# Sums by source in half buckets side by side, and another order of the node steps at the stages' ends

## The chip, the cores and the metric

The kernel runs on one core of a Trainium2 chip. The metric is the time of one execution on the device in microseconds, the median of several runs; lower is better. Names of engines: PE (matrix multiply), DVE (vector), ACT (scalar), POOL (gathers and scatters by index), SP (issues the plain DMAs, in order).

## The reference

Four graph layers follow each other on the same 6250 nodes (rows of 160 numbers: 64 scalars and 32 three-vectors) and the same 100000 edges (`src`, `dst`, sorted by `dst`). Every layer normalizes the node rows, mixes them linearly, forms a message for each edge from the row of one end and from weights that a small network makes of the edge's features, sums the messages over the edges of each node, mixes the sums and adds them to the rows. Layers 0, 1 and 3 read the row of `src` and sum by `dst`. Layer 2 does the opposite, it reads the row of `dst` and sums by `src`, and the edges aren't sorted by `src`:

```python
xs = s[dst]; xv = v[dst]
out0a = w0 * xs                              # and four more products
tp = jnp.concatenate([out0a, out0b, out1a.reshape(E, -1), out1b.reshape(E, -1), out1c.reshape(E, -1)], axis=-1)
agg = jax.ops.segment_sum(tp, src, num_segments=N) / DENOM
```

## The kernel before

The program runs through these stages, one after the other.

- **The start** (lines 740 to 880): the node rows are normalized and mixed for layer 0, in 50 tiles of 128 rows (`nodes_in`). Beside it the sort by `src` begins: `src_b` holds each edge's bucket, `src // 120`, and for each of the 53 buckets (and one for the padding) `count_bucket` (L760, L763) compares `src_b` with the bucket's number and counts, on DVE and partly on ACT (L765). From the counts come `start2`, where each bucket begins, and `off`. A flag tells whether the data keep within what the fast program is made for (among others no more than 16 x 128 edges in a bucket); only if not, the plain program `general` runs instead.
- **`edges(0)`, `edges(1)`, `edges(3)`**, the layers that sum by `dst`: 784 tiles of 128 edges, 4 to a group, so 196 groups. For each tile POOL gathers 128 rows of a table in DRAM by index (L1278), six groups ahead. PE makes the edge weights, DVE the one-hot matrices `oh` (128 edges x 64 nodes) and the messages, and PE sums them, `pg += oh.T @ msg` (L1395): the tiles of a window of 14 alternate between the upper and lower 64 rows of `pg`. A window ends with a chain of node steps, a Python generator that is advanced twice a group: `nodes_out` (transpose, output weights, add to the row), then `nodes_in` of the next layer (norm, transpose, input weights), whose row goes to the next layer's table in DRAM (L1033). The generators that are left after the last group are run one after the other. The first gather of a layer needs the whole table of that layer.
- **The sort's second half**, `positions`, another generator, which `edges(0)` and `edges(1)` advance by one step in every third group: for each bucket DVE makes `hit` (L1165), a running count over it (L1167) and takes it over where it hits (L1170). At its end `edge_to` holds for each edge its place in the order by `src`.
- **`messages2`**: layer 2's messages for each edge. PE spreads the rows of `dst` over the edges (L1482) and makes the weights, DVE forms the products, and POOL scatters each edge's record of 390 numbers to its place in `rec2` in DRAM (L1514). Before that, `tail` (L1424, L1426) writes zeros to 2048 rows behind the last edge, in four DMAs of SP, since the last buckets' loads reach beyond it.
- **`sums2`**: layer 2's sums. A bucket has 120 nodes and 16 slots of 128 records (the last one 10 nodes and 2 slots), read from `rec2` from the bucket's start on, 4 slots a load (L1575, 8 loads ahead, 12 buffers). For each slot DVE makes `oh` (128 x 120, L1606) and two products (L1610, L1612); PE does `pg += oh.T @ [record, products]` in two matmuls of 192 and 288 columns (L1616, L1618). Records of a neighbouring bucket that a load takes in match no column of `oh`. Each bucket's node steps follow (`nodes_out`, then `nodes_in` of layer 3).

Instructions are placed on each engine in an order that the framework's scheduler chooses; each engine works its own list in order, and so does SP with its DMAs, those that load and those that write.

Of the kernel before, what the change touches and what calls it, by code (L numbers as in the profile page):

```python
# [66 lines left out]
BN = 120  # L67
BK = (N + BN - 1) // BN
LASTN = N - (BK - 1) * BN
S = 16  # L70
LASTS = 2
EP = TT * P + S * P

# [616 lines left out]
class Fast:  # L690
# [5 lines left out]
    def __init__(self, tc, a, out, shared, dram):  # L696
# [6 lines left out]
        self.rec2 = dram.tile([EP, RW], F32, name="rec2")  # L703
# [3 lines left out]
    def prologue(self):  # L707
# [16 lines left out]
        self.start2 = sh.tile([1, BK], I32, name="start2")  # L724
# [5 lines left out]
        self.zeros_b = sh.tile([P, TT], BF16, name="zeros_b")  # L730
# [21 lines left out]
        nc.vector.tensor_scalar(flt, src, 1.0 / BN, 0.5 / BN - 0.5, op0=ALU.mult, op1=ALU.add)  # L752
        nc.vector.tensor_scalar(flt, flt, 12582912.0, None, op0=ALU.add)
        nc.vector.tensor_scalar(self.src_b, flt, 12582912.0, None, op0=ALU.subtract)
        count = pro.tile([P, BK + 1], F32, name="count")

        def count_bucket(b):
            hit = pro.tile([P, TT], BF16, name="hit", bufs=4)
            if b % 2:
                nc.vector.tensor_scalar(hit, self.src_b, float(b), None, op0=ALU.is_equal, op1=ALU.add,  # L760
                                        accum_out=count[:, b : b + 1])
            else:
                nc.vector.tensor_scalar(hit, self.src_b, float(b), None, op0=ALU.is_equal)  # L763
                junk = pro.tile([P, TT], BF16, name="junk", bufs=2)
                nc.scalar.activation(junk, hit, AF.Copy, accum_out=count[:, b : b + 1])  # L765

        with tc.tile_pool(name="nodes0", bufs=2) as wk, \
# [3 lines left out]
            for b in range(N0 + 4):  # L771
# [14 lines left out]
                if b < BK + 1:  # L786
# [5 lines left out]
        po = pro_ps.tile([P, 2, BK + 1], F32, name="ps_off")  # L792
        nc.tensor.matmul(po[:, 0, :], lhsT=self.before, rhs=count, start=True, stop=True)
        nc.tensor.matmul(po[:, 1, :], lhsT=self.ones, rhs=count, start=True, stop=True)
        total = pro.tile([P, BK + 1], F32, name="total")
        nc.vector.tensor_copy(total, po[:, 1, :])
        ends = pro.tile([P, BK + 1], F32, name="ends")
        nc.vector.tensor_tensor_scan(ends, total, self.zeros_b[:, : BK + 1], 0.0, op0=ALU.add, op1=ALU.add)
        nc.vector.tensor_sub(ends, ends, total)
        nc.vector.tensor_copy(self.start2, ends[0:1, :BK])  # L800
        nc.vector.scalar_tensor_tensor(self.off, ends, -1.0, po[:, 0, :], op0=ALU.add, op1=ALU.add)
# [47 lines left out]
        bad = pro.tile([1, 2, P], F32, name="bad")  # L849
# [7 lines left out]
        nc.vector.tensor_scalar(bad[:, 1, 64 : 64 + BK - 1], total[0:1, : BK - 1], float(S * P), None, op0=ALU.is_gt)  # L857
        nc.vector.tensor_scalar(bad[:, 1, 64 + BK : 65 + BK], total[0:1, BK - 1 : BK], float(LASTS * P), None,
                                op0=ALU.is_gt)
# [281 lines left out]
    def positions(self, wk):  # L1141
# [10 lines left out]
        nc.scalar.copy(rs[:, :, 0:3], sq)  # L1152
        yield
# [9 lines left out]
        for b in range(BK + 1):  # L1163
            hit = wk.tile([P, TT], BF16, name="hit2", bufs=2)
            nc.vector.tensor_scalar(hit, self.src_b, float(b), None, op0=ALU.is_equal)  # L1165
# [6 lines left out]
        nc.vector.tensor_copy(to, pos)  # L1172
# [30 lines left out]
    def edges(self, li):  # L1203
# [179 lines left out]
        for i, (u, g) in enumerate(groups):  # L1383
# [17 lines left out]
            live = [n for n in live if not (next(n, True) or next(n, True))]  # L1401
            if li < 2 and i % 3 == 0:
                next(self.sort, None)
        for n in live:
            for _ in n:
                pass
# [5 lines left out]
    def messages2(self):  # L1412
# [10 lines left out]
        tail = wk.tile([P, 4, RW], F32, name="tail", bufs=1)  # L1423
        nc.vector.memset(tail, 0.0)  # L1424
        for r in range(TT * P, EP, 4 * P):
            nc.sync.dma_start(self.rec2[r : r + 4 * P, :].rearrange("(p r) c -> p r c", r=4), tail)  # L1426
# [121 lines left out]
    def sums2(self):  # L1548

        nc, tc, li = self.nc, self.tc, 2  # L1550
        es = ExitStack()
        ld = es.enter_context(tc.tile_pool(name="ld_s", bufs=12))
# [7 lines left out]

        def slots(b):
            return S if b < BK - 1 else LASTS

        data, xts, starts = {}, {}, {}
        groups = [(b, g) for b in range(BK) for g in range(0, slots(b), G)]

        def load(b, g):

            m, n = min(G, slots(b)), BN if b < BK - 1 else LASTN
            if g == 0:  # L1570
                starts[b] = nc.values_load(
                    self.start2[0:1, b : b + 1], engines=[mybir.EngineType.SP], min_val=0, max_val=E,
                    skip_runtime_bounds_check_because="a count of edges, of which there are E")
            rt = ld.tile([P, G, RW], F32, name="rt")
            nc.sync.dma_start(rt[:, :m, :],  # L1575
                              self.rec2[ds(starts[b] + g * P, m * P), :].rearrange("(p s) c -> p s c", s=m))
            loc = ld.tile([P, G], F32, name="loc")
            nc.vector.tensor_scalar(loc[:, :m], rt[:, :m, 261], float(-BN * b), None, op0=ALU.add)
            data[b, g] = rt, loc
            if g == 0:  # L1580
                rows = slice(1 + BN * b, 1 + BN * b + n)
                xt = nk.tile([BN, XW], F32, name="xt", bufs=8)[:n]
                nc.sync.dma_start(xt, self.x[2][rows, :])
                sk = nk.tile([BN, 192], F32, name="sk_out", bufs=8)[:n]
                nc.sync.dma_start(sk, self.skip[2][rows, :])
                xts[b] = xt, sk
# [179 lines left out]
```

## Time and profile before

| | us |
|---|---|
| runs of the kernel before (3) | 5309.66 median, 5302.54 to 5310.14 |
| the profiled execution, its own time | 5299.63 |
| its span, first to last instruction | 5297.8 |
| start, until the first gather of layer 0 | 172.0 |
| `edges(0)`, first to last gather | 172.0 to 1213.5 |
| `edges(1)`, first to last gather | 1270.8 to 2304.9 |
| `messages2`, first scatter to the first load of `sums2` | 2369.0 to 3429.8 |
| `sums2`, first load to the last sum matmul | 3429.8 to about 4234.8 |
| `edges(3)`, first to last gather | 4255.8 to 5270.8 |

Over the span PE is busy 83%, DVE 78%, POOL 60%, ACT 39%; the mean clock granted to PE is 0.880. These shares are means over stages with different limits, so the stages are read one by one. Each fp32 matmul stands in the records twice (834 slots of `sums2` give 1668 records of L1618).

### The profile page before, as it was taken

The page shows a single profiled execution, that of the slowest core. Times are in us where ns is not written, and L with a number is a line of the kernel's source. Part 1 is how long each engine was busy: PE and PEld are TensorE (multiplying, and loading weights), DVE is VectorE, ACT ScalarE, POOL GpSimd, SP SyncE. Part 2 cuts the span into 40 slices and gives each one's busy share as a digit, 9 for nine tenths or more (in the row PEclk, how much of TensorE's full clock was granted, in tenths as well). Part 3 has the DMA queues.
Part 4 walks back from the last instruction along what each step waited for, and adds up shares of the span by engine and source line. Part 5 has one row for each costly group of instructions (what it writes and reads, how often), then busy time and mean ns, then how long its engine had stood idle before and what let it go on. Part 6 is the DMA issues. An engine that isn't in the chain of part 4 may idle for free. (4 is left out here: it accounts for less than half of the span.)

```text
span 5297.8 us, 77181 instructions
## 1 busy us (share of the span) xinstructions
PE 4419.6 (83%) x22084; PEld 2768.0 (52%) x22084; DVE 4113.6 (78%) x11512; ACT 2078.7 (39%) x6858; POOL 3199.1 (60%) x3143
## 2 busy tenths in 40 slices
PE   6899999998999999965555556499999988878886
PEld 4455555554555555533333334388888844444443
DVE  6688889896898988857777777577777668887787
ACT  5444445443444545523333333222222244434332
POOL 0577777774777777747777777600000067777776
PEclk9999999997998989977777777699999978898888
DMA  3333333322333333336565555487777433333322
GB/s 96 114 94 95 95 95 92 94 73 78 98 101 96 100 96 99 87 123 209 199 207 199 204 198 198 172 287 234 237 234 237 157 88 83 87 82 85 84 81 58
DMA packets 373004, 708.21 MB, mean 134 GB/s; under 512 B 71469, under 2 KB 250890, under 8 KB 372442
## 3 DMA queue, kind: packets, MB, share of 16 engines
q0 software_dynamic: 163072, 349.43, 21.7%
q1 hardware_dynamic: 208914, 353.42, 21.3%
q8 instruction: 180, 2.95, 0.2%
q14 instruction: 254, 2.08, 0.1%
q10 hardware_dynamic: 584, 0.33, 0.0%
HBM read 493.90 MB, written 209.08 MB: 133 GB/s over the span
## 5 line engine op out<-in xcount | busy, mean ns | idle before, releaser
L1278 POOL DMA_INDIRECT ge<-table,rt x2352 | 2378.3, 1011 | 1770.4 <-DMA skip<-sk 828.2
L1395 PE MATMUL pg<-msg,oh 128*64 128x384 f32 x4704 | 1041.3, 563 | 145.7 <-DVE msg L1339 106.2
L1514 POOL DMA_INDIRECT rec<-row,edge_to x784 | 820.1, 1046 | 301.6 <-issue 187.6
L1305 ACT ACTIVATE ws<-pw,rt 128x96 f32<-128x96 f32 x2352 | 693.1, 350 | 768.9 <-PE pw L1301 265.1
L1301 PE MATMUL pw<-w_w2y,hh 100*128 100x192 f32 x3136 | 675.7, 352 | 17.2 <-ACT ws L1307 14.7
L1395 PEld LDWEIGHTS pg<-msg,oh 128*64 128x64 f32 x4704 | 304.3, 148 | 685.2 <-issue 251.2
L1301 PEld LDWEIGHTS pw<-w_w2y,hh 100*128 100x128 f32 x3136 | 529.7, 200 | 226.3 <-ACT ws L1307 124.8
L1338 DVE TENSOR_TENSOR msg<-msg,bank 128x768 f32<-128x768 f32 x588 | 554.6, 943 | 0.0
L1618 PE MATMUL pg<-msg,oh 128*120 128x288 f32 x1668 | 540.7, 405 | 0.0
L1482 PE MATMUL pe<-tb,oh 64*128 64x160 f32 x1568 | 276.0, 410 | 241.4 <-ACT row L1491 239.2
L1334 DVE TENSOR_TENSOR msg<-ws,ge 128x512 f32<-128x512 f32 x588 | 401.4, 683 | 67.4 <-DMA ge<-table,rt 66.1
L1616 PE MATMUL pg<-rt,oh 128*120 128x192 f32 x1668 | 409.3, 327 | 34.1 <-DVE oh L1606 34.1
L1270 ACT ACTIVATE hh<-ph 100x1024 f32<-100x1024 f32 (+1 forms) x336 | 269.4, 802 | 417.4 <-PE pw L1294 182.6
L1331 DVE TENSOR_TENSOR pr<-ge,bank 128x384 f32<-128x384 f32 x588 | 319.4, 543 | 133.5 <-DMA ge<-table,rt 131.9
L1482 PEld LDWEIGHTS pe<-tb,oh 64*128 64x128 f32 x1568 | 208.6, 255 | 393.0 <-ACT row L1491 384.7
L1307 ACT COPY ws<-pw 128x192 f32<-128x192 f32 x1176 | 391.1, 333 | 0.0
L1267 PE MATMUL ph<-ft,w_w1r 12*100 12x512 f32 (+1 forms) x784 | 337.0, 657 | 57.5 <-ACT hh L1270 40.9
L1616 PEld LDWEIGHTS pg<-rt,oh 128*120 128x120 f32 x1668 | 297.6, 183 | 122.4 <-issue 35.3
L1507 DVE TENSOR_TENSOR row<-pw,ev 128x512 f32<-128x512 f32 x196 | 135.2, 690 | 285.3 <-ACT row L1493 271.0
L1456 PE MATMUL ph<-ft,w_w1d 128*128 128x512 f32 x224 | 170.4, 856 | 220.4 <-ACT hh L1458 197.0
L1332 DVE TENSOR_REDUCE dot<-pr 128x128 f32<-128x384 f32 x588 | 342.8, 583 | 0.1
L1339 DVE TENSOR_TENSOR msg<-ge,ws 128x384 f32<-128x384 f32 x588 | 323.0, 549 | 0.0
(485 smaller groups left out, 7278.8 us busy)
## 6 DMA issues: line engine op xcount, KB each, us to landing
rt<-rec SPq DMA_DIRECT2D x208, 780.0 KB
ge<-table,rt POOLq DMA_INDIRECT x2352
ft<-in_ft_dram SPq DMA_DIRECT2D x56, 512.0 KB
ft<-in_ft_dram SPq DMA_DIRECT2D x28, 896.0 KB
dt<-in_dst_w_dram SPq DMA_DIRECT2D x112, 224.0 KB
xt<-x SPq DMA_DIRECT2D x168, 82.0 KB
rec<-row,edge_to POOLq DMA_INDIRECT x784
rt<-in_rec_dram SPq DMA_DIRECT2D x84, 112.0 KB
```

The lines of the kernel that those rows point to most:

```text
L1278: nc.gpsimd.indirect_dma_start(out=ge[:, k, :], out_offset=None, in_=self.table[li], in_offset=bass.IndirectOffsetOnAxis(ap=rt[:, G * g + ...
L1301: nc.tensor.matmul(pw[:, i, :192], lhsT=hh[:, k + i, :], rhs=w2, start=True, stop=True)
L1305: nc.scalar.activation(ws[:, k0 + i, 0:96], pw[:, i, 0:96], AF.Copy, scale=rt[:, G * g + k0 + i, 0:1])
L1307: nc.scalar.copy(ws[:, k0 : k0 + m, 96:192], pw[:, :m, 96:192])
L1332: nc.vector.tensor_reduce(dot, pr.rearrange("p g c u -> p g u c"), AX.X, ALU.add)
L1334: tt(msg[:, :, AW - 64 : AW + 64].rearrange("p g (k u) -> p g k u", k=2), ws.rearrange("p g (k u) -> p g k u", k=2)[:, :, :, 0:64], e0[:, ...
L1338: tt(mvec[:, :, :, 0:64], by3(t1, 64), yv[:, :, :, None].to_broadcast([P, n, 3, 64]), ALU.mult)
L1395: nc.tensor.matmul(pg[half], lhsT=oh[:, k, :], rhs=msg[:, k, :AW], start=t % WT < 2, stop=t % WT >= WT - 2)
L1482: nc.tensor.matmul(pe[:, 2 * h + k // 2, :160], lhsT=oh[rows, (t0 + k) % WT // 2, :], rhs=tb[rows], start=True, stop=True)
L1514: d = nc.gpsimd.indirect_dma_start(out=self.rec2, out_offset=bass.IndirectOffsetOnAxis(ap=self.edge_to[:, t0 + k : t0 + k + 1], axis=0), i ...
L1616: nc.tensor.matmul(pg[:, 0:192], lhsT=oh[:, k, :], rhs=rt[:, k, 0:192], start=first, stop=end, skip_group_check=True)
L1618: nc.tensor.matmul(pg[:, 192:480], lhsT=oh[:, k, :], rhs=msg[:, k, :], start=False, stop=end, skip_group_check=True)
```

## The change

Sums by source: a bucket has 128 nodes in two halves of 64. Each half has 9 slots of its own, and starts at its own place of `rec2`, so that there are 49 buckets of 2 x 9 slots, read 3 slots of each half at a time, in two loads of 3 slots (before, one of 4). The two halves' one-hot matrices are 64 columns wide, and their matmuls write the upper and lower 64 rows of `pg`. To have both halves counted in one pass over a bucket, each edge counts 1 or 4096 (`src_v`), so the comparison of the sort becomes one of `src_b`, multiplied by `src_v` (`scalar_tensor_tensor` in place of `tensor_scalar`); a few more operations take the two counts apart at the end. The flag's conditions become those of the halves: at most 9 x 128 edges in a half, and a half's start within 500 of 1024 times its number. Since no load reaches beyond the last edge any more (the start is capped), `tail` goes.

At the stages' ends: in the last 12 groups of `edges(0)` and `edges(1)` the sort isn't advanced, in the last 4 groups of every `edges` a node generator is advanced three times in place of two, and the generators left after the last group, in `edges` and in `sums2`, are run in turns.

The diff, cut to its core:

```diff
-BN = 120
-BK = (N + BN - 1) // BN
-LASTN = N - (BK - 1) * BN
-S = 16
-LASTS = 2
-EP = TT * P + S * P
+BK = (N + P - 1) // P
+BH = (N + HN - 1) // HN
+S, SG = 9, 3
+RH = 1024
+DRIFT, BIAS = 500.0, 512.0
+SHIFT = 4096.0
...
-        self.rec2 = dram.tile([EP, RW], F32, name="rec2")
+        self.rec2 = dram.tile([TT * P, RW], F32, name="rec2")
...
+        nc.vector.scalar_tensor_tensor(flt, self.src_b, float(-P), src, op0=ALU.mult, op1=ALU.add)
+        nc.vector.tensor_scalar(flt, flt, float(HN), SHIFT - 1.0, op0=ALU.is_ge, op1=ALU.mult)
+        nc.vector.tensor_scalar(self.src_v, flt, 1.0, None, op0=ALU.add)
...
-            if b % 2:
-                nc.vector.tensor_scalar(hit, self.src_b, float(b), None, op0=ALU.is_equal, op1=ALU.add,
-                                        accum_out=count[:, b : b + 1])
-            else:
-                nc.vector.tensor_scalar(hit, self.src_b, float(b), None, op0=ALU.is_equal)
+            nc.vector.scalar_tensor_tensor(hit, self.src_b, float(b), self.src_v, op0=ALU.is_equal, op1=ALU.mult,
+                                           **(dict(accum_out=count[:, b : b + 1]) if b % 2 else {}))
+            if b % 2 == 0:
...
-            nc.vector.tensor_scalar(hit, self.src_b, float(b), None, op0=ALU.is_equal)
+            nc.vector.scalar_tensor_tensor(hit, self.src_b, float(b), self.src_v, op0=ALU.is_equal, op1=ALU.mult)
...
-            live = [n for n in live if not (next(n, True) or next(n, True))]
-            if li < 2 and i % 3 == 0:
+            left = len(groups) - i
+            live = [n for n in live if not any(next(n, True) for _ in range(2 if left > 4 else 3))]
+            if li < 2 and i % 3 == 0 and left > 12:
                 next(self.sort, None)
-        for n in live:
-            for _ in n:
-                pass
+        while live:
+            live = [n for n in live if not next(n, True)]
...
-        tail = wk.tile([P, 4, RW], F32, name="tail", bufs=1)
-        nc.vector.memset(tail, 0.0)
-        for r in range(TT * P, EP, 4 * P):
-            nc.sync.dma_start(self.rec2[r : r + 4 * P, :].rearrange("(p r) c -> p r c", r=4), tail)
...
-        ld = es.enter_context(tc.tile_pool(name="ld_s", bufs=12))
+        ld = es.enter_context(tc.tile_pool(name="ld_s", bufs=11))
...
+        M = 2 * SG
+        AHEAD = 8
...
-        groups = [(b, g) for b in range(BK) for g in range(0, slots(b), G)]
+        groups = [(b, g) for b in range(BK) for g in range(0, S, SG)]
...
-            rt = ld.tile([P, G, RW], F32, name="rt")
-            nc.sync.dma_start(rt[:, :m, :],
-                              self.rec2[ds(starts[b] + g * P, m * P), :].rearrange("(p s) c -> p s c", s=m))
-            loc = ld.tile([P, G], F32, name="loc")
-            nc.vector.tensor_scalar(loc[:, :m], rt[:, :m, 261], float(-BN * b), None, op0=ALU.add)
+            rt = ld.tile([P, 2, SG, RW], F32, name="rt")
+            for h in range(2):
+                nc.sync.dma_start(rt[:, h], self.rec2[ds(starts[b][h] + g * P, SG * P), :].rearrange(
+                    "(p s) c -> p s c", s=SG))
...
-            oh = wk.tile([P, G, BN], F32, name="oh", bufs=3)
-            tt(oh[:, :n], self.iota[:, None, :BN].to_broadcast([P, n, BN]),
-               loc[:, :n, None].to_broadcast([P, n, BN]), ALU.is_equal)
+            oh = wk.tile([P, 2, SG, HN], F32, name="oh", bufs=3)
+            tt(oh, self.iota.rearrange("p (h n) -> p h n", h=2)[:, :, None, :].to_broadcast([P, 2, SG, HN]),
+               loc.rearrange("p (h s) -> p h s", h=2)[:, :, :, None].to_broadcast([P, 2, SG, HN]), ALU.is_equal)
...
-            for k in range(n):
-                first, end = g + k == 0, g + k == slots(b) - 1
-                nc.tensor.matmul(pg[:, 0:192], lhsT=oh[:, k, :], rhs=rt[:, k, 0:192], start=first, stop=end,
-                                 skip_group_check=True)
-                nc.tensor.matmul(pg[:, 192:480], lhsT=oh[:, k, :], rhs=msg[:, k, :], start=False, stop=end,
-                                 skip_group_check=True)
+            for k in range(SG):
+                first, end = g + k == 0, g + k == S - 1
+                for o, m in ((0, 192), (192, 288)):
+                    for h in range(2):
+                        nc.tensor.matmul(pg[HN * h : HN * h + HN, o : o + m], lhsT=oh[:, h, k, :],
+                                         rhs=(msg if o else rt)[:, h * SG + k, 0:m],
+                                         start=first and o == 0, stop=end, skip_group_check=True)
...
-        for n in live:
-            for _ in n:
-                pass
+        while live:
+            live = [n for n in live if not next(n, True)]
```

## The prediction

> **What bounds the kernel now.** I read first the busy time by stretches of 100 us, one from each kind of stage; the columns are named in the first line.
>
> ```profile
> core 0: us, PE busy (x) PEld busy (x) DVE busy (x) ACT busy (x) POOL busy (x), PEclk, DMA share, GB/s
> 900.00:1000.00 100.00, 94.86 (x490) 55.11 (x488) 90.47 (x262) 49.49 (x157) 77.14 (x76) 0.95 0.33 90
> 2800.00:2900.00 100.00, 56.07 (x324) 38.89 (x322) 71.79 (x154) 34.31 (x103) 77.46 (x75) 0.77 0.60 205
> 3700.00:3800.00 100.00, 100.00 (x536) 84.41 (x535) 72.60 (x218) 21.63 (x84) 0.00 (x0) 1.00 0.71 235
> 4700.00:4800.00 100.00, 82.28 (x424) 42.64 (x425) 81.62 (x243) 40.42 (x144) 76.54 (x78) 0.91 0.31 82
> ```
>
> In the three `edges` stages and in `messages2` POOL shows the same 77%, whatever PE and DVE do. The timeline of POOL tells why:
>
> ```profile
> 1205.60 0.94 POOL L1278 DMA_INDIRECT ge<-table,rt  x1 [0.30 <-DMA ge<-table,rt]
> 1206.85 0.94 POOL L1278 DMA_INDIRECT ge<-table,rt  x1 [0.30 <-issue]
> 1270.76 0.94 POOL L1278 DMA_INDIRECT ge<-table,rt  x1 [55.90 <-PE pw L1301]
> ```
>
> A gather takes 0.94 us and the next follows after 0.30 (no gap within a layer is over 0.32), so 1.25 us a tile and 784 x 1.25 = 980 us a layer. That is the limit there; the third line shows the hole of 56 us between two layers. In `sums2` (the row of 3700) POOL is idle and PE has no free moment at full clock, so PE is the limit. SP's own waits in the stage agree: its loads wait for buffers that PE has not finished with.
>
> ```profile
> SPq L1575 <- PE pg L1616: 335.5, 158, 3.3
> ```
>
> The change works on `sums2` above all, and there on PE. The timeline of PE, first a group of four half-wide sums of `edges`, then the full-wide ones of `sums2`:
>
> ```profile
> 1216.55 1.51 PE L1395 MATMUL pg<-msg,oh 128*64 128x384 f32 x8
> 3700.55 0.49 PE L1616 MATMUL pg<-rt,oh 128*120 128x192 f32 x2
> 3700.88 0.65 PE L1618 MATMUL pg<-msg,oh 128*120 128x288 f32 x2
> 3701.36 0.49 PE L1616 MATMUL pg<-rt,oh 128*120 128x192 f32 x2
> ```
>
> A slot of 480 columns takes 3701.36 - 3700.55 = 0.81 us, 1.69 ns a column. Four half-wide matmuls of 384 columns take 1.51 us, 0.98 ns a column with the pipeline's end included; one after the other they would take 2.6. Those for the upper and the lower rows run side by side.
>
> **The change part by part.**
>
> *`sums2`, PE.* From the first load to the last sum it takes 805 us (3429.8 to 4234.8), about 8 of them the first load's way. 797 us over 52.1 buckets is 15.3 us a bucket: 16 x 0.81 = 12.96 for the sums, 2.3 for the node steps. After: 9 pairs of slots at 0.81 (half of two slots) to 0.94 us (480 x 2 x 0.98 ns). I take 0.81, since 1.51 has the end in it: 7.3 + 2.3 = 9.6 us, at most 10.8, for 49 buckets.
>
> *`sums2`, DVE.* Groups of `sums2` from 3500 to 4180 us, busy us and mean ns of one:
>
> ```profile
> L1610 DVE TENSOR_TENSOR msg<-rt 128x768 f32<-128x768 f32 x178 | 169.4, 951 | 0.0
> L1606 DVE TENSOR_TENSOR oh<-iota,loc 128x480 f32<-128x480 f32 x178 | 116.7, 655 | 75.9 <-PE pg L1618 75.2
> L1612 DVE TENSOR_TENSOR msg<-rt 128x384 f32<-128x384 f32 x177 | 97.6, 551 | 0.0
> L1578 DVE TENSOR_SCALAR loc<-rt 128x4 f32<-128x4 f32 x181 | 29.9, 165 | 94.6 <-DMA rt<-rec 94.1
> ```
>
> Neighbours overlap by about 0.08 us, so a group of four costs 2.32 - 0.32 = 2.0 us and a bucket 8.0; at 73% busy of 15.2 us the node steps have 3.0. After, six slots a group: by the slope between 384 and 768 elements (1.04 ns) the products take 1.35 (1152) and 0.75 us (576), `oh` with 384 elements 0.55 (between 407 ns for 256 in L1320 and 655 for 480), `loc` 0.165; less the overlaps 2.5 us. Three groups and the nodes: 10.5 us a bucket.
>
> *`sums2`, DMA.* Before, 834 slots of 128 x 1560 bytes are 166.5 MB; after, 49 x 18 slots, 176.1 MB. Rows in and out (`xt`, `sk`, `table`, `skip`, `x`) are 6250 x 3360 bytes, 21.0 MB: 197.1 MB. What the DMA engines can do lies between two rows, the queue from 3500 to 4200 us (MB, share of the 16 engines) and ten microseconds in which the first loads are all under way:
>
> ```profile
> q1 hardware_dynamic: 57494, 164.99, 71.0%
> 3450.00:3460.00 10.00, 10.00 (x57) 8.63 (x56) 6.08 (x14) 2.64 (x7) 0.00 (x0) 1.00 1.03 378
> ```
>
> 165 MB in 0.71 x 700 us is 332 GB/s while busy, and 197.1 MB make 594 us, 12.1 a bucket; at 378 GB/s 521 us, 10.6. I take the former, since it has the small rows in it. The page "DMA: Bandwidth & Descriptors" of the Trainium skill (Specifications) gives a core about 358 GB/s of HBM; by that, as an estimate, 551 us. The row of 378 stands above that figure.
>
> So the limit passes from PE (9.6) to the DMA queue (12.1), with DVE (10.5) close by. `edges(0)` shows what such closeness costs: PE 95 and DVE 90% busy, and POOL still keeps its pace, for it runs six groups ahead. Here the loads run eight groups ahead. I add 3% for waits: 12.5 us, 49 x 12.5 + 8 = 620 us. **-185 us**; between 805 - 8 - 49 x 10.6 = -278 (DMA at its burst, DVE no hindrance) and, at 14 us a bucket, -111.
>
> What speaks for 14: PE will not be busy throughout any more, and the granted clock follows. At 56% busy it is 0.77 (2800 us), at 82% 0.91; the waits there are short, about 1.5 us a group. The Trainium skill ("TensorE: Matmul & The Clock Gate", Part 1) halves the clock only after an idle window of about 3.4 us; by that rule PE would stay at 9.6 us a bucket. By the rows a PE wanted for 9.6 of 12.1 us gets some 0.9: 10.7 us, still under 12.1 but with little room.
>
> *`tail`.* SP before the first scatter:
>
> ```profile
> 2327.11 5.56 SPq L1426 DMA_DIRECT2D rec<-tail  x3
> 2334.07 0.30 SPq L1033 DMA_DIRECT2D table<-tb  x1
> 2345.44 4.00 SPq L1426 DMA_DIRECT2D rec<-tail  x1
> 2351.04 0.55 SPq L1445 DMA_DIRECT2D tb<-table  x1
> ```
>
> The last rows of the table stand behind three of these DMAs of 0.8 MB (ACT had them at 2328.9), and the load of that table behind the fourth: 17 us from 2334 to 2351, where 3 would do for a write to land. Without them some 5 + 14 us less, and the scatters start that much earlier: **-20 us** (-10 to -28: in the new order on SP loads for `sums2` stand behind the first ones of `messages2`, about 20 at 0.4 us).
>
> *The sort.* L1165 takes 364 ns 54 times; its successor reads two tensors, like L760 with 953 ns: about 0.95 x 50. DVE's sort grows from 54 x (0.36 + 1.84 + 1.03) = 174 to 50 x 3.82 + 4 for the end = 195 us, over two stages in which POOL waits for nothing: hidden. What is not hidden: gathers last longer beside it. From first to last gather the layers take 1041.5, 1034.1 and 1015.0 us, so the two with the sort 45.6 us more. If that goes with DVE's sort time, +5; if with the number of buckets, -3; if POOL stands still for the whole longer comparison, +30. I take **+5**.
>
> *The stages' ends.* Of the 56 us between layers 0 and 1, some 3.6 are sort operations on DVE amid the drain (one L1167, two L1165, one L1170), and of the last window's 11 node steps one more is done in the loop. **-6** there (-12 to 0). From the last sum to `edges(3)`'s first gather it is 21 us; the last two chains in turns save some steps, but the last bucket has 106 nodes in place of 10: **-4** (-8 to +5). After the last gather (26 us) there is one chain alone: 0.
>
> *The start.* The count's even comparisons grow by 0.6 us x 25, but by the new order 10 of them stand before the first norm on DVE, where 19 stood, and later about one goes with each node tile, whose 2.6 us PE sets. 0 (-3 to +11, if DVE is late after all).
>
> Sum: -185 - 20 + 5 - 6 - 4 = -210 us on the profiled 5299.63, so 5090. The median of the runs is 10 us above that execution: **5099 us**. A measurement of this kernel can tell about 0.2% (10 us) from no change.
>
> **The rivals.**
>
> - *The queue at its burst rate* and DVE without waits, 10.6 us a bucket: 5310 - 278 - 25 = 5007. For it: the row of 378 GB/s. Against: it was seen for 30 us, with large packets alone. Chance 0.10.
> - *Three engines wait for each other*, 14 us a bucket as PE's clock sinks: 5310 - 111 - 25 = 5174. For it: the clock's rows. Against: `edges(0)` keeps its pace. 0.17.
> - *The halves do not run side by side* in matmuls of 192 and 288 columns, since each now comes with a weight load of its own per half. PE then has 18 x 0.81 + 2.3 = 16.9 us, 49 x 16.9 + 8 = 836: +31 in `sums2`, -10 to -25 elsewhere, 5316 to 5331, slower. It decides from 1.5 us a pair on. Against: L1395 does the same with two weight loads and 384 columns. 0.06.
> - *It does something else*: the flag sends the data to `general`. From the inputs I count at most 1128 edges in a half (1152 allowed), and starts 352 below to 125 above 1024 times the number (500 allowed): 0.02, and the time would be far above.
>
> **How the numbers follow.** The forecast (11.5 to 13.2 us a bucket) has 0.65: 5050 to 5135. The range takes in most of the second rival and part of the first: 5030 to 5180. The last two rivals are the slower ones: faster 0.91, the same 0.01, slower 0.08.
>
> **What would show it.** In the changed profile: PE records of the 192- and 288-column matmuls in pairs at half the slot time; PE under 95% busy in `sums2` and a DMA share above 0.9; loads there waited for by DVE; no zero writes before `messages2`, and its first scatter about 20 us nearer to the last gather; 1.25 us a gather unchanged. Wrong would be PE at 100% in `sums2` again, a DMA share still near 0.7, or gathers of 1.4 us beside the sort.

## The result, and the profile after

| | before | after |
|---|---|---|
| median of the runs, us | 5309.76 (5302.54 to 5310.14, 4 runs) | 5248.73 (5243.95 to 5264.31, 4 runs) |
| ratio | | 0.9893, 95% interval 0.987 to 0.9917 |
| span of the profiled execution, us | 5297.8 | 5241.9 |

The change made the kernel faster by 61 us (1.1%), not by 210: outside the range. Stage by stage, from the first and last gathers, scatters, loads and sums in the two traces:

| stage, us | before | after | difference | predicted |
|---|---|---|---|---|
| start, to the first gather | 172.0 | 178.3 | +6 | 0 (-3 to +11) |
| `edges(0)`, first to last gather | 1041.5 | 1083.3 | **+42** | with the next: +5 |
| last gather to first of `edges(1)` | 57.3 | 56.2 | -1 | -6 |
| `edges(1)`, first to last gather | 1034.1 | 1048.1 | **+14** | |
| last gather to first scatter | 64.1 | 56.4 | -8 | -20 |
| `messages2`, first to last scatter | 1057.6 | 1059.0 | +1 | 0 |
| `sums2`, first load to last sum | 805.4 | 697.8 | **-108** | -185 |
| last sum to first gather of `edges(3)` | 21.2 | 15.5 | -6 | -4 |
| `edges(3)`, first to last gather | 1015.0 | 1017.8 | +3 | 0 |

Two terms carry the miss: `sums2` gave 77 us less than predicted, and the layers with the sort cost 51 us more. The gap before the first scatter adds 12. In the experiments below, four of the six groups of runs fell on chips that granted PE a mean clock of 0.76 to 0.78 instead of 0.87 (the kernel before took 6930 to 7110 us there): kernels are compared within a group, and `sums2`, where the clock is near 1 on all of them, across groups too. One execution of the kernel with the zero writes, tried twice below, took 13696 us at a granted clock of 1.0, for a reason that was not found; it counts in that kernel's second median and not in its ratio.

The busy times by stretches, after:

```profile
core 0: us, PE busy (x) PEld busy (x) DVE busy (x) ACT busy (x) POOL busy (x), PEclk, DMA share, GB/s
900.00:1000.00 100.00, 94.20 (x458) 56.95 (x454) 82.75 (x232) 44.70 (x141) 71.22 (x71) 0.88 0.33 88
...
3600.00:4100.00 500.00, 407.78 (x3108) 240.69 (x3102) 367.29 (x994) 111.72 (x453) 0.00 (x0) 0.97 0.78 278
...
4700.00:4800.00 100.00, 88.33 (x430) 46.05 (x426) 81.34 (x248) 40.06 (x142) 76.51 (x78) 0.85 0.34 86
```

In `sums2` (3600 to 4100) nothing is full any more: PE 82%, DVE 73%, the DMA engines 78%. In `edges(0)` (900) POOL has fallen to 71%, 71 gathers in 100 us instead of 76, while in `edges(3)` (4700) it keeps its 77%.

What the change was to do in `sums2` it does. The timeline of PE:

```profile
3801.27 0.49 PE L1645 MATMUL pg<-rt,oh 128*64 128x192 f32 x4
3801.60 0.65 PE L1645 MATMUL pg<-msg,oh 128*64 128x288 f32 x4
3802.08 0.49 PE L1645 MATMUL pg<-rt,oh 128*64 128x192 f32 x4
```

Two slots (twice as many records as before in one line) pass in 3802.08 - 3801.27 = 0.81 us, the time of one before. DVE's operations last what was worked out (1.35, 0.75 and 0.55 us); the groups from 3600 to 4100 us:

```profile
L1637 DVE TENSOR_TENSOR msg<-rt 128x1152 f32<-128x1152 f32 x104 | 140.5, 1351 | 0.0
...
L1639 DVE TENSOR_TENSOR msg<-rt 128x576 f32<-128x576 f32 x104 | 78.2, 751 | 0.0
L1633 DVE TENSOR_TENSOR oh<-iota,loc 128x384 f32<-128x384 f32 x104 | 57.4, 552 | 0.0
```

So the loss is in waiting. DVE's own waits in that stretch stand nearly all at one line, where a node chain reads the product `po`; each has a row of its own, of two kinds (one bucket in four has the longer):

```profile
DVE os__98465 L1119 <- PE po L1100: 4.6, 1, 4.6
...
DVE os__95429 L1119 <- PE po L1100: 2.9, 1, 2.9
```

Together they are 111.2 us in 35 buckets, 3.2 us a bucket: with the 10.3 us that DVE is busy, 13.5 of the bucket's 14.1. In the kernel before the same line had 2.2 us in 500, in rows like this one:

```profile
DVE os__94869 L1100 <- PE po L1081: 0.2, 1, 0.2
```

PE's longest waits after, in the same stretch:

```profile
PE pg L1645 <- DVE oh L1633: 52.6, 61, 1.4
PE po L1098 <- ACT at L1085: 27.9, 35, 1.0
```

The timeline shows how it comes about:

```profile
3808.02 0.46 PE L1098 MATMUL po<-w_osr,at 96*128 96x96 f32 x2 [0.79 <-ACT at L1085]
...
3808.32 0.83 PE L1100 MATMUL po<-w_ovw,at 128*128 128x96 f32 x6
...
3809.19 0.26 DVE L1119 TENSOR_TENSOR os__96119<-po,sk_out 128x96 f32<-128x96 f32 x1 [2.83 <-PE po L1100]
```

The chain is advanced two steps a group, and its third and fourth steps fall into one turn: `po` on PE, then `os_` on DVE. PE comes to `po` only after the group's sums, which wait for DVE's products, and after ACT's copy `at` of the transposed rows (the 27.9 us); DVE stands at `os_` until then, and makes no products for the next group; then PE waits for those (the 52.6 us). The two engines take turns instead of working side by side.

In `edges(0)` the gathers now stop; POOL's timeline:

```profile
753.00 0.95 POOL L1308 DMA_INDIRECT ge<-table,rt  x1 [2.59 <-DVE msg L1367]
800.60 0.94 POOL L1308 DMA_INDIRECT ge<-table,rt  x1 [3.81 <-DVE xt L1059]
```

Gaps over 0.4 us, of which there were none before, make 35 us in that layer (less the usual 0.3 each), all from 670 us on: POOL waits for a gather buffer that DVE has not finished with. In `edges(1)` there are none; its gathers themselves last 14 us more in all.

### The profile page after: what moved, and what is told of

It reads as the page before. It is cut to its first block, busy times and chain, and to the rows that moved or that the text cites. A ratio compares the mean times of both kernels' runs of the same rounds, so it can differ in the third digit from the quotient of the medians.

```text
span 5241.9 us, 77184 instructions
## 1 busy us (share of the span) xinstructions
PE 4238.9 (81%) x22204; PEld 2463.7 (47%) x22204; DVE 4084.8 (78%) x11194; ACT 2066.5 (39%) x6802; POOL 3222.7 (61%) x3143
## 3 DMA queue, kind: packets, MB, share of 16 engines
q1 hardware_dynamic: 220478, 359.82, 21.2%
## 4 chain that ended last, share of the span: by engine, by line
PE 17%; DVE 16%; DMA 12%; POOL 8%; issue 6%; ACT 3%; SPq 0%; ACTq 0%; DVEq 0%; POOLq 0%
DMA rec<-row,edge_to 6%; DMA ge<-table,rt 5%; PE pg L1645 4%; POOL rec L1541 4%; POOL ge L1308 3%; PE pg L1425 3%; PE pw L1331 2%; DVE msg L1368 2%; PE po L1100 1%; DVE msg L1637 1%; DVE row L1534 1%; PE ph L1297 1%; DVE msg L1364 1%; PE pt_out L1080 1%; DVE pr L1361 1%
## 5 line engine op out<-in xcount | busy, mean ns | idle before, releaser
L1331 PEld LDWEIGHTS pw<-w_w2y,hh 100*128 100x128 f32 x3136 | 541.0, 204 | 229.7 <-ACT ws L1337 114.2
L1297 PE MATMUL ph<-ft,w_w1r 12*100 12x512 f32 (+1 forms) x784 | 354.0, 656 | 68.8 <-ACT hh L1300 53.1
L1645 PE MATMUL pg<-rt,oh 128*64 128x192 f32 x1764 | 234.3, 345 | 101.1 <-DVE oh L1633 100.9
L1645 PE MATMUL pg<-msg,oh 128*64 128x288 f32 x1764 | 308.1, 428 | 8.3 <-DVE msg L1639 2.8
L1496 PE MATMUL pw<-w_w2d,hh 64*128 64x224 f32 x1568 | 302.0, 474 | 4.3 <-DVE row L1538 4.1
```

Of the source, the lines that this page charges most:

```text
L1297: nc.tensor.matmul(ph[:, i], lhsT=w1[r : r + K, :], rhs=ft[r : r + K, 4 * P * (j // 2) :][:, : 4 * P], start=True, stop=True)
L1331: nc.tensor.matmul(pw[:, i, :192], lhsT=hh[:, k + i, :], rhs=w2, start=True, stop=True)
L1645: nc.tensor.matmul(pg[HN * h : HN * h + HN, o : o + m], lhsT=oh[:, h, k, :], rhs=(msg if o else rt)[:, h * SG + k, 0:m], start=first and o ...
```

## The experiments

**`sums2`: who waits for whom.** The first run adds an empty step, `yield`, at the head of the node chain of `sums2`, so that `po` and `os_` fall into different turns; the second adds two more between them and gives the chains six PSUM tiles.

```diff
             xt, sk = xts.pop(b)
             n = xt.shape[0]
+            yield
             yield from self.nodes_out(2, ...
```

> The changed kernel with one empty step ahead of each bucket's node steps in sums2, so that the second product of a node chain (po) and the sum that reads it (os_, L1119 in the changed kernel) are no longer issued in the same turn: VectorE's products of one more group stand between them. In the changed kernel a bucket takes 14.3 us, of which VectorE is busy 10.4 and stands 2.8 to 4.6 us a bucket at L1119, waiting for po. Theory A, VectorE waits in line for the node chain: a bucket goes to 11.5 to 12.5 us, sums2 from 698 to 570 to 620 us, VectorE there over 83% busy, the whole 5125 to 5170 us. Rival B, the DMA engines or the falling clock set the 14.3 us: nothing moves, 5240 to 5260 us, 14.3 us a bucket, and the wait shows up at another line.

```diff
-        p_n = es.enter_context(tc.tile_pool(name="p_ns", bufs=3, space=PSUM))
+        p_n = es.enter_context(tc.tile_pool(name="p_ns", bufs=6, space=PSUM))
...
         if li == 2:
+            yield
+            yield
             os_ = wk.tile([n, 192], F32, name="os_")
```

> As the run before, and two more empty steps between po and os_, with six instead of three PSUM tiles for the node steps, so that VectorE may be two groups ahead of TensorE. Theory A: the wait at L1119 goes altogether and a bucket comes to what the busiest of three needs: TensorE's 11.6 us (81% of 14.3), the DMA queue's 11.1 (0.775 of 14.3) or VectorE's 10.4; 11.2 to 12.0 us a bucket, 5110 to 5150 us in all. If one shifted turn is enough, the same as that run within 10 us. Rival B: 5240 to 5260 us again.

Both fell on a chip with the lower clock: 6710.19 us, 0.9696 of before (0.9648 to 0.9743), and 6713.81 us, 0.9705 (0.9665 to 0.9744), so only the stage tells. `sums2` took 625.9 and 611.8 us; in another kernel of that group, whose `sums2` is the changed one's, 697.9. The second was run again where the clock is 0.87:

> The changed kernel with one empty step ahead of each bucket's node steps in sums2, two more between po and os_, and six PSUM tiles for them. On the second chip its sums2 took 612 us against 698. Theory A: the same here, 606 to 618 us, the rest as in the changed kernel, 5150 to 5175 us in all. Rival: what sums2 saves is lost in edges(3), whose first gathers start while the clock is still held down after a fuller sums2: edges(3) over 1030 us.

5158.12 us, 0.9717 (0.9696 to 0.9738); `sums2` 611.3 us, `edges(3)` 1014.3. The rows of that run, from 3600 to 4000 us (stretch, DMA queue, one of DVE's waits):

```profile
3600.00:4000.00 400.00, 353.96 (x2908) 222.27 (x2904) 342.06 (x939) 106.26 (x416) 0.00 (x0) 1.00 0.91 326
```

```profile
q1 hardware_dynamic: 50975, 130.00, 90.3%
```

```profile
DVE os__97690 L1121 <- PE po L1100: 1.2, 1, 1.2
```

No work was added or removed, and the stage became 86 us shorter: DVE stands 1.2 us a bucket instead of 3.2, and the DMA engines go from 0.78 to 0.91. The first run, with the one empty step and no more PSUM tiles, gave 72 of it, so the pairing is the cause, as theory A has it. The wait did not go altogether: 12.3 us a bucket, where 11.2 to 12.0 had been expected. Nothing is full even so (PE 88%, DVE 86%, DMA 91%).

**The same edit in the kernel before.**

> The kernel before with the same empty steps and PSUM tiles in sums2 that took 86 us from the changed kernel. There TensorE was 100% busy in the stage, so VectorE's standing in line cost nothing: sums2 805 +- 5 us and 5300 to 5320 us in all. Rival: the wait cost as much there, sums2 750 us or less.

5305.0 us, 1.0005 (0.9993 to 1.0017); `sums2` 806.0 us, PE 100% busy:

```profile
3600.00:4100.00 500.00, 500.00 (x2677) 420.95 (x2676) 358.91 (x1068) 107.52 (x424) 0.00 (x0) 1.00 0.73 235
```

The pairing of steps cost nothing as long as PE was full. The change made it cost.

**The halves one after the other.** All six slots' matmuls of a group in another order:

```diff
-            for k in range(SG):
-                for o, m in ((0, 192), (192, 288)):
-                    for h in range(2):
+            for h in range(2):
+                for k in range(SG):
+                    for o, m in ((0, 192), (192, 288)):
```

> The changed kernel with its sums in sums2 in another order: of each group all six of the lower half and then all six of the upper, so that the two halves stand one after the other on TensorE. The prediction's third rival by itself. If the gain of the change is that the halves run side by side, TensorE needs 18 x 0.81 + 2.3 = 16.9 us a bucket and is the limit again: sums2 some 836 us against 698, over 97% busy, the whole 5370 to 5390 us where the changed kernel takes 5240. If the gain came from the smaller number of buckets or the smaller masks, sums2 stays under 740 us.

5402.76 us, 1.0194 (1.0177 to 1.0211); `sums2` 849.8 us, PE 90% busy from 3600 to 4200 us. Slower than before: all of the gain is in the halves lying side by side. PE was not over 97% busy as expected. Its waits from 3600 to 4100 us are for ACT's copies in the node chain, and not for DVE (0.2 us in all), although DVE stands up to 6.3 us at `os_`:

```profile
PE pt_out L1078 <- ACT acc L1657: 24.9, 28, 0.9
PE po L1098 <- ACT at L1085: 21.9, 28, 0.8
```

**The sort's longer comparison, alone.** In the kernel before:

```diff
-            nc.vector.tensor_scalar(hit, self.src_b, float(b), None, op0=ALU.is_equal)
+            if b:
+                nc.vector.scalar_tensor_tensor(hit, self.src_b, float(b), self.src_b, op0=ALU.is_equal, op1=ALU.min)
+            else:
+                nc.vector.tensor_scalar(hit, self.src_b, float(b), None, op0=ALU.is_equal)
```

> The kernel before, with only the sort's comparison made a two-tensor operation (scalar_tensor_tensor with the bucket number itself as second operand and min, which leaves the same ones and zeros; bucket 0 keeps the old form), 0.96 instead of 0.36 us, 53 times, 28 + 21 of them beside gathers. Theory S, it is the longer comparison that made the two layers with the sort 42 and 14 us longer in the changed kernel: +14 us in edges(1) and +14 to +42 in edges(0), 5338 to 5366 us. Rival C, those 56 us come from something else (the clock of that execution, the new ends of the loop, other bucket sizes): 5305 to 5320 us.

That group had the lower clock: 6885.94 us, 0.9946 (0.9913 to 0.998), half a per cent faster if anything. There the layers take 1400 to 1550 us in all its kernels, and the gaps between gathers make 370 to 550 us of each: the gathers are far from setting the pace, and nothing can be read for the clock of 0.87. So again, with both kernels unchanged beside it, and this time at 0.87:

> The kernel before, unchanged, for a profile beside those of the next runs. If the chip grants the clock of the first profile (0.87 in the mean): layers of 1041, 1034 and 1015 us from first to last gather, no gap between gathers over 0.32 us, sums2 805 us. If it grants 0.77 as in the runs on the second chip: layers of 1400 to 1550 us, set by TensorE, sums2 again 805 to 808 us.

> The changed kernel, unchanged. Theory S (the longer comparison of the sort lengthens the first two layers): edges(0) and edges(1) are again longer than before's in the same call, by 35 to 45 and by 10 to 18 us where the clock is as in the first profile. Rival C (chance, or the clock of that one execution): edges(0) differs from before's by under 10 us. sums2 698 us in both cases, last gather of edges(1) to first scatter 56 against 64 us.

> The kernel before with only the sort's comparison made a two-tensor operation (0.96 for 0.36 us, 53 times; the same positions). Theory S: edges(0) 20 to 42 us and edges(1) 10 to 16 us longer than before's in this call, 5338 to 5366 us where before takes 5310. Rival C: both within 8 us of before's, 5305 to 5320 us. On the second chip, where TensorE sets the pace of these layers, this kernel took 0.995 of the time of before; there the comparison is expected to cost nothing again.

| us | before | with the longer comparison | after |
|---|---|---|---|
| time | 5306.9 | 5369.56, 1.0123 (1.0106 to 1.014) | 5240.34, 0.9875 (0.9859 to 0.9892) |
| `edges(0)` | 1045.5 | 1074.0 | 1083.1 |
| `edges(1)` | 1041.9 | 1065.6 | 1051.5 |

Theory S: the comparison by itself makes both layers longer, 52 us together where the whole change made them 47 us longer in this group. It goes as predicted from 0.378 to 0.964 us, some 29 us of DVE time beside gathers; nearly twice that was paid. In `edges(1)` (24 us) and in all it is more than had been expected (10 to 16 us, 5338 to 5366 us); why the whole change costs that layer only 10 us here stays open. By the sum of their durations the gathers last only 3 and 5 us longer; the rest is gaps, in which POOL waits for DVE:

```profile
POOL ge L1281 <- DVE bst L990: 21.7, 17, 6.7
...
POOL ge L1281 <- DVE msg L1340: 14.4, 14, 2.6
```

**Was there any room before?** POOL never waited in the kernel before, from which the prediction concluded that DVE's work was hidden. The other end of the same buffers says otherwise. DVE's waits in `edges(0)`, 600 to 1213 us, and in `edges(3)`, 4300 to 5000 us, both of before:

```profile
DVE at L1072 <- ACT at L1068: 40.5, 22, 3.7
DVE xt L1094 <- PE po L1081: 14.7, 22, 1.4
```

```profile
DVE pr L1331 <- DMA ge<-table,rt: 52.5, 53, 3.4
```

In `edges(3)` DVE waits for gathers: they set the pace. In `edges(0)` no wait for a gather stands among DVE's. The time from the end of a group's fourth gather to DVE's first product of that group, out of the trace's records, says how far POOL had got ahead:

| us, at group | 5 | 62 | 119 | 176 |
|---|---|---|---|---|
| before, `edges(0)` | 4.4 | 17.2 | 24.1 | 25.4 |
| before, `edges(3)` | 1.7 | 1.7 | 5.6 | 4.6 |
| after, `edges(0)` | 6.1 | 24.6 | 33.6 | 38.3 |
| longer comparison alone, `edges(0)` | 4.4 | 21.7 | 33.6 | 35.7 |

Before, the loop of DVE, PE and ACT was already slower than the gathers, and the eight gather buffers took up the difference until the layer ended. After, they were full halfway through.

**The ends of the loop.** The changed kernel with the old ends of `edges` (two steps to the last, sort to the last, leftover chains one after the other):

> The changed kernel with the old loop of edges: sort steps to the last group, two node steps a group to the last, and the leftover chains one after the other. Theory: the new ends were worth 1 us between edges(0) and edges(1) (57.3 before, 56.2 after) and little before messages2, so 5245 to 5258 us. Rival: they were worth the predicted 6 us and more at each of three ends, and another loss hid it: 5260 to 5275 us. If the new ends are what lengthened layer 0 (1083 us from first to last gather against 1041), it falls back to some 1045 us and the whole to about 5210 us.

6813.98 us, 0.9854 (0.9812 to 0.9897), at the lower clock; `edges(0)` to `edges(1)` 64.8 us, against 68.1 and 59.6 in the two kernels with the new ends in that group. `edges(0)` took 1421.7 us there, 1404.8 and 1407.7 in those two, so nothing speaks for the new ends as what lengthened it. No effect on the gap can be made out; at 0.87 this was not tried.

**`tail`.** The zero writes put back into the changed kernel:

> The changed kernel with the zero writes of tail put back ahead of messages2 (into rows that nothing reads). The prediction had their removal at -20 us (-10 to -28). In the profiles the gap from edges(1)'s last gather to the first scatter fell only from 64.1 to 56.4 us (65.7 to 56.1 in the second pair). If the writes cost what the prediction says and something else lengthened that gap, it comes to 70 us or more here and the whole to 5255 to 5265 us, where the changed kernel takes 5240. If the rows, skip and dt transfers on SP take the time anyway, the gap is 62 to 67 us and the whole 5245 to 5252 us.

> The zero writes put back into the changed kernel, again beside kernels at a clock of 0.87. At 0.76 the gap before messages2 was 91.3 us with them and 80.6 us in the other kernel of that call without them. If that holds here: a gap of 66 to 68 us against 56, and 5246 to 5256 us in all, 8 to 12 us over the changed kernel in this call.

> The changed kernel, unchanged, beside the two of this call: 5240 us at a clock of 0.87, with 56 us before the first scatter, and 697 to 700 us in sums2; at 0.76 some 0.98 of the time of before, with 80 us before the first scatter.

All at the lower clock: 6930.04 us, 0.9812 (0.9782 to 0.9843), and in the next group 6791.27 us, 0.9804 (0.9749 to 0.9859), beside 6805.0 us, 0.9813 (0.9766 to 0.9859), for the changed kernel. That is too coarse for 10 us, but the gap before the first scatter is 91.3 us with the writes against 80.6 in the other kernel of the group, and 89.7 against 79.9: the writes cost 10 us there, half of what was predicted. At 0.87 only the kernels before and after can be compared, which differ in more: 7.7 us, and 9.6 in the second pair.

**The layers with the sort.** Two edits on top of the kernel of 5158 us. The first makes the sort's steps smaller, the second separates ACT's copy of `at` from DVE's addition to it (L1091, the longest of DVE's waits in `edges(0)`):

```diff
                                        op1=ALU.mult)
+            yield
             cum = wk.tile([P, TT], F32, name="cum", bufs=2)
...
-            if li < 2 and i % 3 == 0 and left > 12:
+            if li < 2 and i % 2 == 0 and left > 12:
```

> The last run of the call before (empty steps in sums2, 5158 us) with the sort's work in smaller bites: comparison and scan in steps of their own, and a step with every second group in place of every third. The same work on VectorE in all. If it is the length of one bite (0.96 + 1.84 us at a time) that makes TensorE wait in edges(0) and edges(1), they come back by 20 to 45 us, 5110 to 5135 us. If it is the amount, since VectorE, TensorE and ScalarE together have nothing to spare in these layers, 5148 to 5168 us.

```diff
         if turn is not None:
+            yield
             if carry[0] is not None:
```

> The kernel of 5158 us with one more empty step in the node chains of edges: between ScalarE's copy of at and VectorE's addition of the carried row to it (L1091 in the changed kernel, where VectorE stands 44 us between 600 and 1250 us and 83 us between 1700 and 2300 us, waiting for the copy L1087). No work is added or taken away. Theory: in edges(0) and edges(1) it is the loop of VectorE, TensorE and ScalarE that sets the pace, not the gathers, so without this wait the gathers no longer stop: edges(0) from 1085 to 1040 to 1055 us, edges(1) from 1054 to 1025 to 1045 us, 5100 to 5130 us. Rival: TensorE at its granted clock sets the pace, 5148 to 5168 us. If gathers set it, the same.

5123.14 us, 0.9655 (0.9633 to 0.9677), and 5141.49 us, 0.9705 (0.9688 to 0.9722). The first is the fastest kernel measured at this clock, some 120 us under the changed one (0.9875 and 0.9893). Against the kernel they are built on (0.9717, of another group at the same clock) `edges(0)` fell from 1085.1 to 1066.3 and 1064.8 us, `edges(1)` from 1053.8 to 1043.8 and 1044.3. By the first, the length of one bite on DVE counts, not only the amount. In the second, DVE's wait at L1091 from 600 to 1250 us went from 43.6 to 27.9 us. Its interval overlaps that of the kernel without it (0.9717), so its gain in all isn't shown; the gaps between gathers did go (none over 0.4 us), but the gathers themselves lasted 22 us longer in all (827 for 805 us), and `edges(0)` did not come to the expected 1055. All three edits together:

> Empty steps in sums2, the sort in smaller bites and the empty step before the addition of the carried row, all three. Alone on top of the first, the second gave 35 us (edges(0) 1085 to 1066, edges(1) 1054 to 1044 us) and the third 17 (1085 to 1065, 1054 to 1044). If both take away the same thing (the loop of VectorE, TensorE and ScalarE falling behind the gathers), together they give no more than until the gathers set the pace: edges(0) 1045 to 1060 us, edges(1) 1030 to 1042 us, 5095 to 5125 us. If edges(0) is at TensorE's own limit, 1060 to 1070 us again and 5120 to 5140 us.

> The kernel with all three edits again, since the chip of the run before granted TensorE a clock of 0.76 to 0.78 and the layers there took 1370 to 1580 us whatever the gathers did. Where the clock is 0.87: if the gathers set the pace again, edges(0) 1045 to 1060 and edges(1) 1030 to 1042 us and 5095 to 5125 us in all; if edges(0) is at TensorE's own limit, 1060 to 1070 us and 5120 to 5140 us.

> The kernel with all three edits once more, for the layers at a clock of 0.87: edges(0) 1045 to 1060 and edges(1) 1030 to 1042 us, 5095 to 5125 us, if the gathers set the pace again; 1060 to 1070 us and 5120 to 5140 us if TensorE does. At 0.77 some 0.927 of the time of before, as in the two runs there.

All three runs met the lower clock: 6533.39, 6442.93 and 6540.3 us, 0.9251 (0.9208 to 0.9294), 0.9282 (0.9228 to 0.9336) and 0.9211 (0.916 to 0.9263), where the changed kernel had 0.9813 (in the group of the second). There `edges(3)`, too, falls, from 1528.8 to 1337.1 us within one group. The gathers do not set its pace at this clock (gaps of 534 and 329 us), and DVE's wait at L1091, from 5200 to 6300 us, goes from 413.5 to 149.7 us, while those at `ang` grow from 55 to 140; that the empty step is the cause is likely, but the edits were not tried apart at this clock. What the three are worth together at 0.87 stays open.

## Why the prediction was wrong, step by step

- **`sums2`, PE and DVE by themselves: right for DVE and for a pair of slots, too low for PE in all.** Pairs of slots at 0.81 us, products at 1.35 and 0.75 us; DVE busy 73.5% of (697.8 - 8) / 49 = 14.1 us is 10.3 us a bucket (predicted 10.5). PE is busy 11.5 (81.6%), not 9.6. The sums by themselves make 8.7 of it, not 7.3: the first pair of a group is drawn out, since `oh` is there 0.66 us before the products, and passes in 1.2 instead of 0.81 us (3800.07 to 3801.27). The node steps make 3.2, not 2.3 (the two overlap a little).
- **`sums2`, DMA: wrong in size; close, but not the limit.** 138.59 MB while 77.5% busy for 500 us is 358 GB/s, not 332; 10.9 us a bucket, not 12.1, and less than PE's 11.5. That DMA engines which are not kept busy move less while busy is not the reason for the low value: with the halves in sequence they are busy less still, and 137.03 MB in 0.639 x 600 us are 357 GB/s. The packets of the loads differ (6240 bytes before, 4680 after); whether it is that was not tested. The figure of 358 that the Trainium skill gives in "DMA: Bandwidth & Descriptors", Specifications, is what both this row and the later 130.00 MB in 0.903 x 400 us (360) show; the row of 378 was a start with loads alone, and after the change 414 passed from 3500 to 3520 us.

```profile
q1 hardware_dynamic: 54672, 138.59, 77.5%
q1 hardware_dynamic: 54162, 137.03, 63.9%
```

(The first line is the changed kernel from 3600 to 4100 us, the second the one with the halves in sequence from 3600 to 4200 us.)

- **`sums2`, waits: this is the step that failed.** "I add 3% for waits" came from `edges(0)`, whose loads run ahead; but the lead of the loads is of no use where DVE and PE wait for each other within one turn of a node chain. Measured: 3.2 us a bucket of DVE standing, and with that cut to 1.2 the stage takes 611 us. That this is close to the predicted 620 is in part luck: a DMA need of 12.1 with 3% for waits was forecast, and 10.9 with 13% more was found. The second rival had the 14 us a bucket, and a total of 5174 by it, but for another reason: it let the clock sink to 0.9 at this load. The clock stayed at 0.97, and the longest waits of PE there are 1.4 us. The rows of the other stages did not carry over, and one was misread: in the 100 us of `messages2` at 0.77 PE's waits are not short, five of them are over 3.4 us and the longest is 6.5. The rule of the Trainium skill that the prediction set beside these rows ("TensorE: Matmul & The Clock Gate", Part 1: an idle window of about 3.4 us halves the clock) comes close here, as it would give 1.0. It does not hold to the letter: the trace has the clock at half eight times, for 3.4 us each, in these 500 us, and `edges(3)` before is at 0.87 from 4300 to 5200 us where PE's longest wait is 2.7 us.
- **The sort: the step that failed in the other direction.** The operations lasted what was predicted, DVE's sort time grew by the predicted 20 us or so, but "two stages in which POOL waits for nothing: hidden" was a wrong reading, and so was that `edges(0)` keeps its pace because POOL runs six groups ahead: DVE's lag grew from 4 to 25 us there, and a tile took 1041.5 / 783 = 1.33 us in the mean, not 1.25. Bounded at +30, it cost +56 (47 in the second pair). The bound asked how long POOL could stand still during a comparison, not what happens once a DVE that is already behind falls further back: the gather buffers are full, and its delay is POOL's.
- The Trainium skill ("SBUF — State Buffer", Who interferes with whom) says that a two-input operation of DVE contends with a GpSimd instruction that reads SBUF. The gathers that overlap a long comparison do last longer (40 of them at 1.17 us in `edges(0)` and 23 at 1.43 in `edges(1)` of the second profile of after, where others last 1.02 to 1.03). But that is 40 x 0.14 + 23 x 0.40 = 15 us, and in `edges(1)` of the kernel before the 21 beside the short one-input comparison last 1.22 us already. By the sums of their durations the gathers last 11 us longer than before; the other 36 of the 47 are gaps.
- **`tail`: half of it.** The writes cost 10 us, not 20. What stood behind them on SP is still there; SP after the change:

```profile
2393.11 0.31 SPq L1052 DMA_DIRECT2D table<-tb  x1
2393.67 7.86 SPq L1065 DMA_DIRECT2D skip<-sk  x1
2401.77 3.64 SPq L1066 DMA_DIRECT2D x<-xt  x1
2405.46 4.01 SPq L1473 DMA_DIRECT2D dt<-in_dst_w_dram  x1
2410.48 3.42 SPq L1472 DMA_DIRECT2D tb<-table  x4
```

From the table's last write to its first read it is again 17.4 us (17.0 before): `skip` and `x` of the same node step take 11.5 of them, as they did before (6.85 + 3.67), and a load `dt` the place of the last zero write. The prediction took all of the 17 us but 3 for the writes' doing; its lines of SP leave out `skip` and `x`, which stand between 2334.07 and 2345.44.
- **Ends and start:** -1 for -6 between the layers, -6 for -4 before `edges(3)`, +6 at the start within its bounds. Small; the run with the old ends could not tell what they are worth.
- **The third rival** was refuted by the timeline, and the run with the halves in sequence gave its price: 849.8 us against the predicted 836.

By the measured terms the sum is -108 + 56 - 8 - 1 - 6 + 6 + 3 + 1 = -57, against 55.9 between the two spans.

## What to carry to other kernels

When a change takes the load off the one full engine, look at the steps in which two in-order engines hand work to each other within one turn: their waits were free before and are the new limit. Empty steps between producer and consumer (with more PSUM tiles to hold what is under way) cost nothing in the kernel before and gave 86 us here. That an engine with a queue of buffers never waits does not make it the limit: ask at the other end whether the consumer ever waits for it, and whether its lag grows.

## What had not been expected of the hardware

- The kernel before took 5300 to 5310 us on some chips and 6930 to 7110 on others, at a mean granted clock of 0.88 and 0.76. Of the changed kernel `sums2`, at a clock of 0.97 on both, took the same within 1 us (697.8 and 698.8), while `edges(0)` took 1083 and 1417 us. Why the clock differs there was not found.
- At the start of `sums2`, from 3500 to 3520 us, 414 GB/s passed at a DMA share of 1.02; in the steady stage it was 358 to 360 while busy.
